# A two-layer graph kernel on one core: layer 1 on pairs of blocks

## The chip, the core and the metric

The kernel runs on one core of a Trainium2 chip. A core has five engines that work side by side, each through its own queue in order: TensorE (PE, matrix products, with the load of the stationary operand listed as PEld), VectorE (DVE), ScalarE (ACT), GpSimd (POOL) and SyncE (SP), which here only starts transfers. Engines wait for one another through semaphores. The metric is the device time of one execution in microseconds (us), as the median of the runs shown; lower is better. Everything is in float32.

## The reference, cut to what is computed

128 graphs have 128 nodes each with 256 features. Layer 0 works on all nodes, layer 1 only on the first 25.

```python
h = relu(layernorm(x))
x = x + L0(h, adj)          # convolution over nodes, neighbour sum, gated unit (GRU)
h = relu(layernorm(x))
x = x + L1(h, adj)

def L1(x, adj):             # groups of 25, 9, 7, 6 and 6 nodes
    fused = 0
    for g, idx in enumerate(GROUPS):
        A = adj[idx, idx] + I
        An = deg(A)**-0.5 * A * deg(A)**-0.5
        h = relu(An @ (x[:, idx] @ W1[g]) + b1[g])      # 256 -> 512
        o = relu(An @ (h @ W2[g]) + b2[g])              # 512 -> 256
        fused[:, idx] += softmax(fusion_w)[g] * o
    return fused
```

The five groups have 25 + 9 + 7 + 6 + 6 = 53 nodes (`NR`); a row of layer 1 is one node of one group of one graph. Since `An @ (x @ W1)` equals `(An @ x) @ W1`, the kernel multiplies with `An` first.

## The kernel before

Layer 0 comes in stages. Stages a and b make the convolution through a short Fourier transform (lines up to 573), in two batches of 64 graphs, with the neighbour sums beside them. Then `stage_c(q)` computes the gates of group q, four graphs at a time, q from 0 to 31 (line 730 on; nearly all its matmuls are recorded at line 758). It ends in `turned` and `returned` (925, 935), which write the new x to DRAM (`x1d`, line 941) from POOL's queue. `fetch(q)` (946) reads the first 32 nodes of these graphs back into `x1` and copies the other nodes to the output.

Layer 1 works on blocks of 16 graphs (`SB`), four groups of q, so there are eight blocks (`NBLK`).
- `rows(q)` (1000) makes the normalized rows `x1h` of four graphs: statistics on VectorE, the power -0.5 on POOL, the subtraction on VectorE, the ReLU on ScalarE.
- `prepare(blk)` (1019) loads the small adjacency, normalizes it and leaves it in two shapes: `ac` for the second use of `An` and `r4` for the first.
- `block(blk)` (1082) does the rest. For each of its four q it multiplies `x1h` with `r4` (`py`, 1094) and evicts into `yz`, which holds the features on the partitions and the rows as columns: half by VectorE (1096), half by ScalarE (1097). For each group g, `first(g)` multiplies 16 x n columns of `yz` with W1 (1111; 8 matmuls, evicted by ScalarE with bias and ReLU at 1113 into `hh`), and `second(g)` multiplies `hh` with W2 (1120; 8 matmuls, copied back over `yz` by VectorE at 1122). So the matmuls of the five groups are 400, 144, 112, 96 and 96 columns wide.
- Its tail is `turn(q)`, `gather(q)` and `fuse(q)` for each q. `turn` transposes `yz` back (1142) and ScalarE copies it into `zt` (1146). `gather` multiplies with `ac` in quarters of the array (1154), VectorE adds the bias row (1157), ScalarE applies the ReLU (1158). `fuse` sums the groups with their weights (1164), VectorE adds that to `x1` (1166), and a DMA writes the output: from POOL's queue (1169), for the last block in pieces from SP and two from ACT (1173).
- W1 of one group (512 KB) is loaded by `load_w1` (996) from SP's queue into one of two buffers, two groups ahead of its use. W2 stays.

The order of instructions on all engines is fixed when the program is built, by `Order` (179): programs yield the cost of the step just recorded on TensorE and a time to stay away; lanes with weights are interleaved by these planned costs. Sets such as `C_DONE`, `R_DONE`, `PY_DONE`, `P_DONE`, `B1_DONE` and `F_DONE` hold a program back in this plan only. On the chip each engine takes its instructions in that order and waits for semaphores of data and of buffers. Layer 1 is one lane (`second`, 1209) with weight 0.2: `prepare` and `block` of each block in turn, two running at a time. When the last gates are done, what is left of that lane follows. The tiles that pass through PSUM under the tag `tmp` share five banks (`ptmp`, 221).

For q = 31 the way is shorter: the result is transposed on TensorE (`po`, 902) and added to `x1` directly (904), without DRAM between.

## Time and profile before

| | |
|---|---|
| median of 3 runs | 1995.26 us (1993.5 to 1996.35) |
| the profiled execution's own time | 1999.49 us |
| span in the profile (first to last instruction) | 1997.7 us |
| mean granted clock of TensorE | 0.998 |
| gates of layer 0 (`p`, line 758), share of the chain that ended last | 40% |
| products with W1 (1111) | 640 records, 107.9 us busy |
| products with W2 (1120) | 640 records, 107.3 us busy |
| `gather` (1154), `fuse` (1164) | 256 records, 21.4 us; 128 records, 20.8 us |
| load of W1 (998) | 40 transfers of 512 KB |

A float32 matmul appears as two records on TensorE. [...] the spacing of starts says what a matmul takes of TensorE's time. In a line of the waits, the waiting instruction stands first, then what it waited for, then total us, times and the longest. In a line of the order of time, the start stands first, then the modelled busy time of the merged instructions. A name such as `pz<-hh,w` is the output and the inputs, followed by partitions x elements.

### The profile page before, as it was taken

Reading aid. Unit: us, or ns where it says so; the run is one execution under the profiler, and the core shown is the slowest. Engines: PE = TensorE matmul, PEld = TensorE weight load, DVE = VectorE, ACT = ScalarE, POOL = GpSimd, SP = SyncE. Lnnn points to the kernel's source line nnn. Section 1 sums busy time; section 2 is a strip of 40 time slices with the busy share of each in tenths; the row PEclk is TensorE's granted clock in tenths of the full one; section 3 lists DMA queues with packets and bytes.
Section 4 is the critical chain, followed back from the end, with each engine's and each line's share of the span. In section 5 each row is a group of like instructions: output and inputs, shape, how many; then the busy total and the mean of one; then the engine's idle time right before and its main releaser. Section 6 shows DMA issues by size and latency. Waiting matters only on the chain.

```text
span 1997.7 us, 33167 instructions
## 1 busy us (share of the span) xinstructions
PE 1950.6 (98%) x12486; PEld 1610.6 (81%) x12486; DVE 1349.5 (68%) x3042; ACT 683.2 (34%) x1547; POOL 650.1 (33%) x898
## 2 busy tenths in 40 slices
PE   7999999999999999999999999999999999999998
PEld 5667888889888888878778878878888888887865
DVE  6775445875433566885885887778678867886652
ACT  3664222444222344222323322232323322322233
POOL 3553665333665111240321233122221321322320
PEclk9999999999999999999999999999999999999999
DMA  9998778654877643542434343443433533433332
GB/s 207 300 283 274 259 265 283 204 164 152 274 254 254 193 127 106 162 106 80 116 95 108 111 111 84 114 109 95 120 110 82 127 105 98 109 101 98 77 90 57
DMA packets 184106, 302.89 MB, mean 152 GB/s; under 512 B 28501, under 2 KB 131994, under 8 KB 183690
## 3 DMA queue, kind: packets, MB, share of 16 engines
q1 hardware_dynamic: 138762, 168.82, 29.1%
q0 software_dynamic: 44800, 131.66, 23.1%
q8 instruction: 99, 1.62, 0.4%
q14 instruction: 61, 0.50, 0.1%
q10 hardware_dynamic: 384, 0.28, 0.1%
HBM read 204.13 MB, written 109.05 MB: 157 GB/s over the span
## 4 chain that ended last, share of the span: by engine, by line
PE 86%; DVE 6%; DMA 4%; issue 1%; ACT 1%; POOL 1%; SPq 0%; DVEq 0%; POOLq 0%; ACTq 0%
PE p L758 40%; PE pa L534 7%; PE ph L1111 5%; PE pm L645 5%; PE pz L1120 5%; PE pc L425 4%; PE pb L534 3%; PE pf L436 3%; PE px L671 3%; PE pi L715 2%; PE pw L480 1%; PE ph L414 1%; PE py L1094 1%; PE pg L1154 1%; PE pse L629 1%
## 5 line engine op out<-in xcount | busy, mean ns | idle before, releaser
L941 POOL DMA_DIRECT2D x1d<-xt x128 | 101.1, 815 | 418.8 <-DVE xt L939 418.4
L840 POOL DMA_DIRECT2D xt<-in_x x128 | 100.2, 790 | 175.4 <-DMA x1d<-xt 168.3
L566 DVE SCALAR_TENSOR_TENSOR y<-pa,kk 128x512 f32<-128x512 f32 x78 | 53.8, 690 | 151.4 <-ACT kk L565 151.4
L534 PE MATMUL pa<-wf,X 128*128 128x256 f32 x640 | 152.2, 381 | 0.0
L758 PE MATMUL p<-th,wrz 128*128 128x256 f32 x512 | 135.4, 387 | 0.0
L758 PE MATMUL p<-tm,wrz 128*128 128x256 f32 x512 | 131.9, 380 | 0.0
L758 PE MATMUL p<-tc,wrz 128*128 128x256 f32 x512 | 131.4, 379 | 0.0
L534 PEld LDWEIGHTS pa<-wf,X 128*128 128x128 f32 x640 | 118.1, 190 | 16.2 <-issue 2.0
L425 PE MATMUL pc<-c1w,hTa 128*128 128x256 f32 x512 | 121.0, 382 | 1.2 <-ACT hTa L416 1.2
L645 PE MATMUL pm<-wmsg,hT 128*128 128x256 f32 x512 | 121.5, 382 | 0.0
L758 PEld LDWEIGHTS p<-th,wrz 128*128 128x128 f32 x512 | 95.1, 191 | 18.7 <-issue 6.3
L1111 PE MATMUL ph<-yz,w 128*128 128x96 f32 (+3 forms) x640 | 107.9, 322 | 1.8 <-DVE yz L1096 1.3
L758 PEld LDWEIGHTS p<-tm,wrz 128*128 128x128 f32 x512 | 97.8, 191 | 13.5
L425 PEld LDWEIGHTS pc<-c1w,hTa 128*128 128x128 f32 x512 | 94.0, 190 | 18.1 <-DVE h L428 4.8
L758 PEld LDWEIGHTS p<-tc,wrz 128*128 128x128 f32 x512 | 97.3, 190 | 14.0 <-issue 1.0
L645 PEld LDWEIGHTS pm<-wmsg,hT 128*128 128x128 f32 x512 | 95.8, 190 | 15.2 <-ACT kk L565 1.4
L727 ACT ACTIVATE xc<-xc,t_bn 128x256 f32<-128x256 f32 x128 | 58.1, 501 | 145.9 <-DVE xc L724 145.9
L1120 PE MATMUL pz<-hh,w 128*128 128x96 f32 (+3 forms) x640 | 107.3, 322 | 0.0
L1111 PEld LDWEIGHTS ph<-yz,w 128*128 128x128 f32 x640 | 86.8, 190 | 22.9 <-issue 15.0
L1113 ACT ACTIVATE hh<-ph,vec 128x96 f32<-128x96 f32 (+3 forms) x160 | 63.2, 401 | 120.5 <-PE ph L1111 111.7
L1120 PEld LDWEIGHTS pz<-hh,w 128*128 128x128 f32 x640 | 86.3, 191 | 17.6
L758 PE MATMUL p<-hTc,wrz 128*128 128x256 f32 x384 | 99.2, 381 | 1.1 <-DVE z L832 1.1
(207 smaller groups left out, 4433.6 us busy)
## 6 DMA issues: line engine op xcount, KB each, us to landing
wf<-wfd SPq DMA_DIRECT2D x160, 256.0 KB
wfd<-ws POOLq DMA_DIRECT2D x64, 320.0 KB, 9.0
yd<-y POOLq DMA_DIRECT2D x80, 256.0 KB, 4.1
yt<-yd SPq DMA_DIRECT2D x64, 320.0 KB
w<-in_W SPq DMA_DIRECT2D x40, 512.0 KB
xa<-in_x SPq DMA_DIRECT2D x128, 128.0 KB
hTd<-hTa POOLq DMA_DIRECT2D x32, 512.0 KB, 6.7
hT<-hTd SPq DMA_DIRECT2D x32, 512.0 KB
```

Source lines behind the costliest of these rows:

```text
L425: nc.tensor.matmul(pc[:, i], hT[:, k, (2 * h + i) * N:(2 * h + i + 1) * N], c1w[:, k], start=(k == 0), stop=(k == 1))
L436: nc.tensor.matmul(pf[:, i, :F * NB], h1[:, 2 * h + i, k * P:(k + 1) * P], fwd, start=True, stop=True)
L534: nc.tensor.matmul(ps, xk(k), WF[f][:, k, s], start=(k == 0), stop=(k == 1))
L645: nc.tensor.matmul(pm[:, i], hT[:, k, j * N:(j + 1) * N], LATE["wmsg"][:, k], start=(k == 0), stop=(k == 1))
L671: nc.tensor.matmul(px[:, dc, i], msgs[h][:, i, dc * P:(dc + 1) * P], aT[:, 2 * h + i], start=True, stop=True)
L727: nc.scalar.activation(xc[:, co, s], xc[:, co, s], AF.Relu, bias=sft["bn2"][:, co:co + 1])
L758: nc.tensor.matmul(ps[:, m], w[:, i, k, m * P:(m + 1) * P], factor(i, x, t), start=first and j == 0, stop=last and j == len(n) - 1, skip_g ...
L840: nc.gpsimd.dma_start(out=xt[a * WIDE:(a + 1) * WIDE].rearrange("p b d c -> p (b d) c"), in_=slices(x[q * GB:(q + 1) * GB])[a])
L941: nc.gpsimd.dma_start(out=slices(x1d[q])[a], in_=xt[a * WIDE:(a + 1) * WIDE].rearrange("p b d c -> p (b d) c"))
L1111: nc.tensor.matmul(ph, w1[:, k, m * P:(m + 1) * P], yz[:, k, :, o:o + n], start=(k == 0), stop=(k == 1))
L1113: nc.scalar.activation(hh[:, m], ph, AF.Relu, bias=v("b1", g * 4 + m))
L1120: nc.tensor.matmul(pz, w2[:, g, m, cc * P:(cc + 1) * P], hs[g][:, m], start=(m == 0), stop=(m == 3))
```

## The change

Layer 1 goes over pairs of blocks, 32 graphs. The groups of 25 and 9 nodes are still multiplied for 16 graphs at a time, for the first half of the pair and then for the second. The groups of 7, 6 and 6 nodes are multiplied once for all 32 graphs, 224, 192 and 192 columns wide, after the second half's rows are in (`TURNS` and `plan`). A pair loads a W1 seven times, where two blocks loaded ten. `yz` holds 32 graphs. The hidden rows `hh` and the turned-back rows `zt` share one tile `hz`, cut in three ways for each. The tail runs once for both blocks: eight `turn`, and four `gather` and four `fuse` that each take two groups of q, eight graphs, at once, with 512 columns in an addition, a ReLU and a fusing matmul. There are three `ac` buffers for two, six `x1h` buffers for eight. The lane runs three programs at a time with weight 0.18. In the last block the output's pieces go 12 from SP and 4 from ACT.

```diff
-        S["ac"] = [pool.tile([P, SB // 2, RP], FP, name=f"ac{i}") for i in range(2)]
+        S["ac"] = [pool.tile([P, SB // 2, RP], FP, name=f"ac{i}") for i in range(3)]
...
-        S["yz"] = pool.tile([P, 2, SB, RP], FP, name="yz")
+        S["yz"] = pool.tile([P, 2, 2 * SB, RP], FP, name="yz")
+        S["hz"] = pool.tile([P, 3, 2 * QS // 4, 2, D], FP, name="hz")
...
-        for t in (*r4, S["yz"][:, 0], S["yz"][:, 1], S["b1"], S["aj"]):
+        for t in (*r4, S["yz"][:, 0, :, NR:], S["yz"][:, 1, :, NR:], S["b1"], S["aj"]):
...
+    TURNS = [(g, h * SB, SB) for h in range(2) for g in range(2)]
+    TURNS += [(g, 0, 2 * SB) for g in range(2, NG)]
+
     def load_w1(n):
 
-        if n < NBLK * NG:
+        if n < NBLK // 2 * len(TURNS):
             S["w1", n] = S["pool"].tile([P, 2, HID], FP, tag="w1", name=f"w1_{n}", bufs=2)
-            nc.sync.dma_start(out=S["w1", n], in_=W1[n % NG].rearrange("(k p) o -> p k o", p=P))
+            nc.sync.dma_start(out=S["w1", n], in_=W1[TURNS[n % len(TURNS)][0]]
+                              .rearrange("(k p) o -> p k o", p=P))
...
-        while not (q in C_DONE and -1 in P_DONE and (q < 8 or q - 8 in PY_DONE)):
+        while not (q in C_DONE and -1 in P_DONE and (q < 6 or q - 6 in PY_DONE)):
...
-        x1h = S["x1h", q] = S["pool"].tile([P, D], FP, tag="x1h", name=f"x1h{q}", bufs=8)
+        x1h = S["x1h", q] = S["pool"].tile([P, D], FP, tag="x1h", name=f"x1h{q}", bufs=6)
...
-        while not (blk - 1 in P_DONE and blk - 2 in {-2, *B1_DONE}):
+        while not (blk - 1 in P_DONE and blk - 3 in {-3, -2, *B1_DONE}
+                   and (blk < 2 or (blk - 1) * QS - 1 in PY_DONE)):
             yield 0.0, 1.0
         pool, pool2, b1 = S["pool"], S["pool2"], S["b1"]
-        ac, r4 = S["ac"][blk % 2], S["r4"][blk % 2]
+        ac, r4 = S["ac"][blk % 3], S["r4"][blk % 2]
...
-    def block(blk):
-        while not (blk in P_DONE and blk - 1 in B1_DONE):
+    def pair(pr):
+        b0 = 2 * pr
+        while not (b0 in P_DONE and (not pr or b0 - 1 in F_DONE)):
...
-        pool, yz, b2row = S["pool"], S["yz"], S["b2row"]
-        w2, ac, r4 = S["w2"], S["ac"][blk % 2], S["r4"][blk % 2]
...
+        yz, b2row, w2, hz = S["yz"], S["b2row"], S["w2"], S["hz"]
+        hf = hz.rearrange("p s i a d -> p (s i a d)")
+        space = [hf[:, :4 * SB * SIZES[0]], hf[:, 4 * SB * SIZES[0]:4 * SB * sum(SIZES[:2])],
+                 hf[:, 4 * SB * sum(SIZES[:2]):]]
+        hs = {}
...
+        def first(i, where):
+            g, s, nb = TURNS[i]
             n, o = SIZES[g], OFFS[g]
-            w1 = S.pop(("w1", blk * NG + g))
-            hh = hs[g] = pool.tile([P, 4, SB, n], FP, tag="hh0" if g == 0 else "hh",
-                                   name=f"hh{blk}_{g}", bufs=1 if g == 0 else 2)
+            w1 = S.pop(("w1", pr * len(TURNS) + i))
+            hh = hs[i] = space[where][:, :4 * nb * n].rearrange("p (m b n) -> p m b n", m=4, n=n)
...
-                ph = ptmp.tile([P, SB, n], FP, tag="tmp", name=f"ph1{blk}_{g}_{m}")
+                ph = ptmp.tile([P, nb, n], FP, tag="tmp", name=f"ph1{pr}_{i}_{m}")
...
-                                     yz[:, k, :, o:o + n], start=(k == 0), stop=(k == 1))
+                                     yz[:, k, s:s + nb, o:o + n], start=(k == 0), stop=(k == 1))
...
-        def second(g):
+        def second(i):
...
-                pz = ptmp.tile([P, SB, n], FP, tag="tmp", name=f"pz1{blk}_{g}_{cc}")
+                pz = ptmp.tile([P, nb, n], FP, tag="tmp", name=f"pz1{pr}_{i}_{cc}")
...
-                    nc.tensor.matmul(pz, w2[:, g, m, cc * P:(cc + 1) * P], hs[g][:, m],
+                    nc.tensor.matmul(pz, w2[:, g, m, cc * P:(cc + 1) * P], hs[i][:, m],
...
-                nc.vector.tensor_copy(yz[:, cc, :, o:o + n], pz)
-
-        for g in range(NG + 1):
-            if g < NG:
-                first(g)
-                yield 5.5 if g == 0 else 1.95, 0.0
-            if g:
-                second(g - 1)
-                yield 5.5 if g == 1 else 1.95, 0.0 if g < NG else 1.0
-            if g < NG:
-                load_w1(blk * NG + g + 2)
-        x1 = X1[blk]
...
+                nc.vector.tensor_copy(yz[:, cc, s:s + nb, o:o + n], pz)
+
+        cost = [max(0.112, nb * SIZES[g] * 0.00084) * 16 for g, _, nb in TURNS]
+        plan = [[(0, 0), (1, 1)], [(2, 0), (3, 1), (4, 2), (5, 0), (6, 2)]]
+        for half in range(2):
+            while b0 + half not in P_DONE:
+                yield 0.0, 0.5
+            for q in range(half * QS, half * QS + QS):
+                yield from rows_in(q)
+            ahead = None
+            for i, where in plan[half]:
+                first(i, where)
+                yield cost[i], 0.0
+                if ahead is not None:
+                    second(ahead)
+                    yield cost[ahead], 0.0
+                load_w1(pr * len(TURNS) + i + 2)
+                ahead = i
+            second(ahead)
+            yield cost[ahead], 1.0
...
-            zt = zts[q] = pool.tile([P, 2, D], FP, tag="zt", name=f"zt{blk}_{q}", bufs=4)
-            nc.scalar.activation(zt, pz, AF.Copy)
-
-        def gather(q):
-            zt = zts[q]
-            pg2 = [ptmp.tile([P, D], FP, tag="tmp", name=f"pg2{blk}_{q}_{s}") for s in range(2)]
-            for a in range(2):
-                for s in range(2):
-                    rows = slice(s * RP, (s + 1) * RP)
-                    nc.tensor.matmul(pg2[s][a * RP:(a + 1) * RP], ac[rows, 2 * q + a],
-                                     zt[rows, a], start=True, stop=True)
+                        yz[:, cc, b:b + 2, :].rearrange("p s r -> p (s r)"), ident)
+            nc.scalar.activation(hz[:, q // 2 % 3, q % 2], pz, AF.Copy)
+
+        def gather(h):
+            zt, ac = hz[:, h % 3], S["ac"][(b0 + h // 2) % 3]
+            pg2 = [ptmp.tile([P, 2, D], FP, tag="tmp", name=f"pg2{pr}_{h}_{s}")
+                   for s in range(2)]
+            for i in range(2):
+                for a in range(2):
+                    for s in range(2):
+                        rows = slice(s * RP, (s + 1) * RP)
+                        nc.tensor.matmul(pg2[s][a * RP:(a + 1) * RP, i],
+                                         ac[rows, 4 * (h % 2) + 2 * i + a],
+                                         zt[rows, i, a], start=True, stop=True)
             for s in range(2):
-                nc.vector.tensor_add(zt[:, s], pg2[s], b2row)
-            nc.scalar.activation(zt, zt, AF.Relu)
-
-        def fuse(q):
-            zt = zts.pop(q)
-            pf = ptmp.tile([P, D], FP, tag="tmp", name=f"pfu{blk}_{q}")
+                nc.vector.tensor_add(zt[:, :, s], pg2[s],
+                                     b2row[:, None, :].to_broadcast([P, 2, D]))
+                nc.scalar.activation(zt[:, :, s], zt[:, :, s], AF.Relu)
+
+        def fuse(h):
+            zt, blk = hz[:, h % 3], b0 + h // 2
+            x1 = X1[blk][:, 2 * (h % 2):2 * (h % 2) + 2]
+            pf = ptmp.tile([P, 2, D], FP, tag="tmp", name=f"pfu{pr}_{h}")
             for s in range(2):
-                nc.tensor.matmul(pf[s * 2 * WIDE:(s + 1) * 2 * WIDE], s2w, zt[:, s],
+                nc.tensor.matmul(pf[s * 2 * WIDE:(s + 1) * 2 * WIDE], s2w, zt[:, :, s],
                                  start=True, stop=True)
-            nc.vector.tensor_add(x1[:, q], x1[:, q], pf)
-            b0 = blk * SB + q * GB
-            if blk < NBLK - 1:
-                nc.gpsimd.dma_start(out=out[b0:b0 + GB, :WIDE], in_=x1[:, q])
-                return
-            for j in range(GB):
-                eng = nc.scalar if q == QS - 1 and j % 2 else nc.sync
-                eng.dma_start(out=out[b0 + j, :WIDE], in_=x1[j * WIDE:(j + 1) * WIDE, q])
-
-        for what, q in ((turn, 0), (turn, 1), (turn, 2), (gather, 0), (turn, 3), (gather, 1),
-                        (gather, 2), (fuse, 0), (gather, 3), (fuse, 1), (fuse, 2), (fuse, 3)):
-            what(q)
-            if (what, q) == (gather, QS - 1):
-                B1_DONE.add(blk)
-            yield {turn: 0.45, gather: 0.5, fuse: 0.5}[what], 0.5
-        F_DONE.add(blk)
+            nc.vector.tensor_add(x1, x1, pf)
+            for i in range(2):
+                g0 = (b0 * QS + 2 * h + i) * GB
+                if blk < NBLK - 1:
+                    nc.gpsimd.dma_start(out=out[g0:g0 + GB, :WIDE], in_=x1[:, i])
+                    continue
+                for j in range(GB):
+                    eng = nc.scalar if h % 2 and j % 2 else nc.sync
+                    eng.dma_start(out=out[g0 + j, :WIDE], in_=x1[j * WIDE:(j + 1) * WIDE, i])
+
...
+        for what, i in ((turn, 0), (turn, 1), (turn, 2), (gather, 0), (turn, 3), (turn, 4),
+                        (gather, 1), (turn, 5), (fuse, 0), (gather, 2), (turn, 6), (turn, 7),
+                        (fuse, 1), (gather, 3), (fuse, 2), (fuse, 3)):
+            what(i)
+            if what is gather and i % 2:
+                B1_DONE.add(b0 + i // 2)
+            if what is fuse and i % 2:
+                F_DONE.add(b0 + i // 2)
+            yield {turn: 0.45, gather: 1.0, fuse: 1.0}[what], 0.5
 
...
-    second = [setup_1()] + [part(blk) for blk in range(NBLK) for part in (prepare, block)]
+    second = [setup_1()]
+    for pr in range(NBLK // 2):
+        second += [prepare(2 * pr), prepare(2 * pr + 1), pair(pr)]
...
-              Lane(second, ahead=2, weight=0.2))
+              Lane(second, ahead=3, weight=0.18))
```

## Prediction

> **What bounds the kernel now.** I read the page first, then the waits of TensorE, then stretches of the run, then single stretches in order of time.
>
> ```profile
> span 1997.7 us, 33167 instructions
> ## 1 busy us (share of the span) xinstructions
> PE 1950.6 (98%) x12486; PEld 1610.6 (81%) x12486; DVE 1349.5 (68%) x3042; ACT 683.2 (34%) x1547; POOL 650.1 (33%) x898
> ```
>
> TensorE (PE) is busy for 98% of the span and the next engine for 68%. So matmul time that goes shortens the run, and work saved on the other engines does not. The stretches below (length, then busy time by engine) show where there is any slack: none between 1400 and 1800 us, where gates of layer 0 and pieces of layer 1 alternate, and 13 us in the last 95 us, where layer 1 is alone.
>
> ```profile
> 1400.00:1600.00 200.00, 199.02 (x1257) 164.96 (x1256) 152.80 (x338) 59.20 (x130) 54.05 (x77) 1.00 0.42 109
> 1600.00:1800.00 200.00, 200.00 (x1303) 166.71 (x1305) 155.09 (x337) 59.35 (x129) 48.35 (x71) 1.00 0.38 102
> 1903.00:1997.70 94.70, 81.65 (x534) 57.23 (x533) 38.23 (x106) 32.13 (x73) 14.84 (x26) 0.98 0.26 72
> ```
>
> TensorE's waits (total, times, longest) are small; no load of the gate stage or of W1 is among them.
>
> ```profile
> PE p L758 <- DVE r L880: 7.1, 8, 2.4
> ...
> PE py L1094 <- ACT x1h L1015: 2.0, 1, 2.0
> ...
> PE py L1094 <- DVE x L1166: 1.1, 1, 1.1
> ...
> PE po L902 <- DVE zr L896: 0.9, 1, 0.9
> ```
>
> "Busy" does not say how fast, so I take prices from start to start in the order of time. This is block 7, alone at the end (start, modelled busy time):
>
> ```profile
> 1964.14 5.54 PE L1120 MATMUL pz<-hh,w 128*128 128x400 f32 x16
> 1969.52 1.95 PE L1111 MATMUL ph<-yz,w 128*128 128x112 f32 x16
> 1971.30 2.13 PE L1120 MATMUL pz<-hh,w 128*128 128x144 f32 x16
> 1973.26 1.92 PE L1111 MATMUL ph<-yz,w 128*128 128x96 f32 x16
> 1975.02 1.96 PE L1120 MATMUL pz<-hh,w 128*128 128x112 f32 x16
> 1976.82 1.96 PE L1111 MATMUL ph<-yz,w 128*128 128x96 f32 x16
> 1978.61 3.72 PE L1120 MATMUL pz<-hh,w 128*128 128x96 f32 x32
> ```
>
> Each product is two records. One record of 400 columns costs 5.38/16 = 0.336 us, of 144 columns 1.96/16 = 0.1225, of 112 columns 1.78/16 = 0.111, of 96 columns 1.76/16 = 0.110. In the gates, 256 columns cost 0.864/4 = 0.216 (starts 1786.58, 1787.44). From 144 to 400 the price is a line of 0.00083 us a column; below 128 it is flat at 0.11. The three small groups lie on the flat.
>
> **Part 1, the three small groups on 32 graphs.** Before, one block spends 1.78 + 1.80 (7 nodes) and 1.76 + 1.79 + 3.57 (twice 6 nodes) = 10.7 us, a pair 21.4. After, a pair has 32 records of 224 columns and 64 of 192. No row shows these widths; they lie between rows of 144 and 256, so the line gives 0.189 and 0.163: 6.05 + 10.43 = 16.5. That is 4.9 us a pair, **19.7 us** over four, all on the engine that bounds.
>
> [...] I take the trace: 19.7.
>
> The groups of 25 and 9 nodes keep their width (400 and 144): nothing. ScalarE and VectorE lose instructions: 96 evictions of hidden rows at 0.34 to 0.35 become 48 of about 0.43, and 48 copies of 0.26 to 0.28 become 24: some 16 us on engines with room, counted at nothing. W1 is loaded 28 times instead of 40; what its wait holds up on SP's queue are loads that TensorE never waited for, so fewer of them gain nothing either.
>
> **Part 2, the tail on two groups of four graphs at once.** Rows for it:
>
> ```profile
> 1903.80 1.09 PE L1154 MATMUL pg<-zt,ac 64*64 64x256 f32 x16
> 1904.82 0.65 PE L1164 MATMUL pfu<-zt,s2w 128*64 128x256 f32 x4
> ```
>
> One gather costs 0.59 from start to start, two in a row 1.02. One fuse costs 0.58, of which its columns are 2 x 0.216 = 0.43 and 0.15 is the change of tiling. A fuse of 512 columns has no row: between 0.86 (columns alone) and 1.16 (two of before); nearest is 0.86 + 0.15 = 1.01. A pair: 8 x (0.59 + 0.58) - 4 x (1.02 + 1.01) = 1.2 us, times four = 5.0. Between gates, the first product behind a gather or a fuse takes 0.54 where others take 0.43 (1900.84, 1901.43, 1901.97); a pair has eight fewer such returns: 0.9, for the three pairs that lie among gates 2.6. Together **7.6 us**.
>
> **Part 3, what becomes late at the end.** Before, layer 1 lagged two blocks: when the last gate product ended (1903.7), blocks 6 and 7 were still to do, and block 6 hid the way of the last rows (q = 31) into layer 1. In the order of the changed program, after the last gate product stand the second products of block 6's groups 0 and 1, `pr` of block 7, then `py_4`, `py_5`, `po`, `py_6`, `py_7`, and only then block 7's groups. Block 7's rows are wanted at once. I follow the queues, t = 0 at the last gate product:
> - TensorE: `pz` 400 wide to 5.4, `pr` to 6.4, `pz` 144 wide to 8.4.
> - VectorE in order: the copy of that 400-wide product ends at 6.1, because the finish of dc = 1 (3 x 0.72) is queued behind it: 8.2; four copies of `r4` at 0.38: 9.7; two copies: 10.3; the finish of dc = 0: 12.4; `zr`: 12.8.
> - So `py_4` starts at 9.9 rather than 8.4, `po` at 12.95. Behind `po`: its addition (14.0), a copy, statistics (0.42 + 0.18 + 0.15), the power on POOL with its way (0.86, from 1915.49 to 1916.35), subtraction 0.40, ReLU 0.42: `py_7` at 17.1, the first product of block 7 at 18.5. TensorE's work in it is 11.6: **6.9 us idle**. Before, the same rows waited 0.4 + 1.15 + 0.9 + 1.25 + 0.5 = 4.2.
>
> The last tail: `turn`, `gather` and `fuse` of two blocks without gates between. On ScalarE the copy of turn 3 stands behind both ReLUs of gather 0 (copy and ReLU 0.53 to 0.63, addition of 512 columns 0.60 to 0.69, as L875 and L1158 have them). Stepping through: gather 1 ends at 6.2 after the first turn, gather 2 at 9.4, gather 3 at 13.05, the last fuse at 15.6 with 11.75 of work: 3.9 idle, where one tail of before had 1.1 (8.20 - 7.13 from 1982.0 to 1990.2).
>
> ```profile
> 1987.91 7.60 SPq L1173 DMA_DIRECT2D out<-x  x14
> ```
>
> The run ends by SP: 14 output DMAs at 0.54 us, then 2.2 to the end of the span. After, SP issues 12, none before fuse 2 of block 7 is added (15.0): 15.0 + 12 x 0.54 + 2.2 = 23.8, so 8.2 behind the last matmul instead of 7.5.
>
> Sum of idle time: 6.9 + 3.9 + 8.2 = 19.0 against 13.0 (94.7 - 81.65): **+6.0 us**.
>
> **Part 4, waits among the gates.** In the new order a pair's second half asks for its rows one group of gates apart (groups 14 to 17, 24 to 25), so these groups carry little of layer 1 between their last, short products. Where gates had little beside them before, `p` waited 0.59 to 0.67 for `r` (834.59, 867.87, 1003.99). Some four such groups: 2.4. Bounds: 0 (the wait is met elsewhere) to 8 (a wait of 2 for `x1h`, as seen once, at four more `py`). I take **+2.5**, near the rows. The new waits of `prepare` (three `ac`, six `x1h`) hold only plan time; SP's and POOL's orders keep their count of loads per group.
>
> **Sum**: -19.7 - 7.6 + 6.0 + 2.5 = **-18.8 us**. The profiled execution (1999.49, span 1997.7) would be 1980.7; it stands 4.2 above the median of the runs, so I forecast 1995.26 - 18.8 = **1976.5 us**.
>
> **Rivals.**
> - *The end costs more*: the power or the ReLU queued later, and the clock. [...] Between `py_6` (14.1) and `py_7` (17.1) lie 3.0 us. In the trace, 1.25 us of idle left the clock at 1.00, and it shows 0.78 only in the last 7.5 us, without matmuls. [...] I take nothing. With it, a tail 3 us longer and Part 4 at 6: 1985. Chance 0.15.
> - *More gained*: gates hide Part 4, a fuse costs 0.86, the end 4: about 1971. Chance 0.12.
> - *No change*: [...] Against it: 96 and 112 columns cost the same. Chance 0.05.
> - *Slower*: rows come late. A pair's second half needs rows just made; TensorE is in order, so a `py` that waits holds every gate behind it. Twelve such `py` in three pairs at the 1.95 us seen at 1049.76 make 23.4: 1976.5 - 2.5 + 23.4 = 1997.4; at 2.5 us, 2004. It decides from about 1.8 us each. Against it: from `xt` added (1885.17) to the row in place is 15.9 us (issue at 1896.42, 4.6 to landing), plus 2.5 to the ReLU, while the plan leaves 24.5; and the same pattern in block 1 (`py_1` to `py_3`, one a group, before 1000 us) shows no wait. Chance 0.07.
>
> The forecast keeps 0.61. A measurement of this kernel tells some 0.2%, 4 us, from no change; faster by more than that 0.88, within 0.05, slower 0.07. Range: costs at their good ends (-2.5, -2, -2.4) and run scatter give 1968; the first rival with scatter 1988.
>
> **What would show it.** Records of 192 and 224 columns start every 0.163 and 0.189 us; 16 fuses at 1.0; `p` behind `r` L880 at about 10 us in total; waits of `po` and `py` near 7 us after the last gate; the span ends 8 us after the last matmul. I am wrong if the small groups of a pair still take over 20 us, or if `py` behind `x1h` sums to over 15 us.

## The result, and the profile after

| | before | after |
|---|---|---|
| median of 22 runs each, side by side | 1999.01 us (1993.5 to 2004.56) | 1993.56 us (1985.45 to 1999.38) |
| ratio after / before | | 0.9961, 95% interval 0.9949 to 0.9972 |
| span of the profiled execution | 1997.7 us | 1991.4 us |
| mean granted clock of TensorE over the runs | 0.9969 (93 runs) | 0.9947 (28 runs) |

The changed kernel is 5.5 us faster by the medians, 7.8 us by the ratio. The forecast was 18.8 us. (The 93 runs of the kernel before are those beside the experiments; 28 are the 22 and 6 more.)

The head of the page after the change: TensorE has 448 records fewer and still bounds.

```profile
span 1991.4 us, 32103 instructions
## 1 busy us (share of the span) xinstructions
PE 1935.7 (97%) x12038; PEld 1595.8 (80%) x12038; DVE 1341.2 (67%) x2970; ACT 670.8 (34%) x1499; POOL 651.3 (33%) x898
```

The stretches (length, then busy time of PE, PEld, DVE, ACT and POOL, then the granted clock, DMA share, GB/s):

```profile
1400.00:1600.00 200.00, 198.60 (x1244) 163.94 (x1243) 149.14 (x319) 60.90 (x129) 55.89 (x80) 1.00 0.39 101
1600.00:1800.00 200.00, 199.82 (x1207) 168.40 (x1205) 144.27 (x310) 56.78 (x123) 43.44 (x63) 1.00 0.37 101
1903.00:1991.40 88.40, 72.12 (x378) 50.78 (x376) 32.25 (x67) 25.17 (x52) 9.29 (x14) 0.96 0.23 63
```

Between 1400 and 1800 us TensorE stays full. Alone at the end it is idle for 88.4 - 72.1 = 16.3 us instead of 13.0, and the clock of that stretch is 0.96 instead of 0.98. The waits of TensorE (total us, times, longest):

```profile
PE p L758 <- DVE r L880: 5.4, 10, 0.7
...
PE py L1105 <- ACT x1h L1020: 5.3, 3, 2.8
...
PE pg L1172 <- ACT hz L1162: 2.0, 3, 1.0
...
PE py L1105 <- DVE r L1084: 1.4, 1, 1.4
...
PE po L902 <- DVE zr L896: 1.3, 1, 1.3
```

`py` behind `x1h` has grown from 2.0 to 5.3 us: 2.8 of it is the last `py` of the run, 1.95 is the wait that was there before. The gates' wait for `r` at L880 came ten times for 5.4 us; before it came eight times for 7.1, of which a single wait was 2.4.

The small groups of the last pair, in the order of time:

```profile
1947.66 3.61 PE L1121 MATMUL ph<-yz,w 128*128 128x224 f32 x16
...
1953.07 2.76 PE L1121 MATMUL ph<-yz,w 128*128 128x192 f32 x16
1955.67 3.19 PE L1131 MATMUL pz<-hz,w 128*128 128x224 f32 x16
1958.69 3.63 PE L1121 MATMUL ph<-yz,w 128*128 128x192 f32 x16
1962.15 5.37 PE L1131 MATMUL pz<-hz,w 128*128 128x192 f32 x32
```

Rows have 16 records, the last 32; the distance to the next start gives the price (1951.11 and 1967.36 follow the first and the last row). The second products (`pz`) cost 3.02/16 = 0.189 us at 224 columns and 5.21/32 = 0.163 at 192: the forecast to the digit. The first products (`ph`) do not: 224 columns cost 3.45/16 = 0.216; of two groups with 192 columns, one costs 2.60/16 = 0.163 and the other 3.46/16 = 0.216. All records of a form, with their busy time and mean ns:

```profile
L1121 PE MATMUL ph<-yz,w 128*128 128x192 f32 x128 | 25.6, 353 | 0.0
L1131 PE MATMUL pz<-hz,w 128*128 128x192 f32 x128 | 21.9, 326 | 0.0
L1121 PE MATMUL ph<-yz,w 128*128 128x224 f32 x64 | 14.4, 378 | 0.0
L1131 PE MATMUL pz<-hz,w 128*128 128x224 f32 x64 | 12.8, 352 | 0.0
```

The same numbers of records, the same columns and the same weights' size: `ph` takes 3.7 + 1.6 = 5.3 us more than `pz`. (A record's mean, 326 to 378 ns, is longer than the spacing of starts, 163 to 216 ns: records overlap.)

To see where the rest went I added up both traces from start to start on TensorE, every gap over 0.1 us counted as idle (us; "gates" are the records of line 758):

| | forecast | before | after | measured |
|---|---|---|---|---|
| all products with W1 and W2 | -19.7 | 203.5 | 190.1 | -13.4 |
| `gather` and `fuse` | -5.0 | 38.0 | 33.3 | -4.7 |
| gates (cheaper returns behind a `gather` or `fuse`) | -2.6 | 894.3 | 895.0 | +0.7 |
| idle among gates | +2.5 | 13.1 | 16.3 | +3.2 |
| idle after the last gate, and the end behind the last matmul | +6.0 | 13.5 | 16.9 | +3.4 |
| first gate to end of span, with all the rest | -18.8 | 1322.6 | 1310.4 | -12.2 |
| start to first gate | 0 | 675.1 | 681.0 | +5.9 |

(The terms hold what the clock took in their stretch.) Up to the first gate the two programs issue the same instructions on every engine, in the same order. What differs ahead of it in these two executions is when two transfers came in, and windows of 3.41 us at half clock: the trace before has one such window ahead of its last matmul, at 779 us; the trace after has five, at 171, 372, 785, 1041 and 1932 us. Two of the five lie ahead of the first gate, and two among the gates, where the trace before has its one.

The difference ahead of the first gate may be more than chance. In the three kept profiles of the kernel before (one with its rows placed, as told below) the first gate starts at 674.1 to 675.4 us and no window at half clock lies ahead of it. In the eleven profiles of the changed kernel and its variants it starts at 675.8 to 683.2 us, behind one to four such windows. No run here shows why.

### The profile page after: what moved, and what is told of

The parts are those of the page before. It is cut to its first block, busy times and chain, and to the rows that moved or that the text cites. A ratio compares the mean times of both kernels' runs of the same rounds, so it can differ in the third digit from the quotient of the medians.

```text
span 1991.4 us, 32103 instructions
## 1 busy us (share of the span) xinstructions
PE 1935.7 (97%) x12038; PEld 1595.8 (80%) x12038; DVE 1341.2 (67%) x2970; ACT 670.8 (34%) x1499; POOL 651.3 (33%) x898
## 4 chain that ended last, share of the span: by engine, by line
PE 85%; DVE 9%; DMA 2%; ACT 1%; issue 1%; SPq 0%; POOL 0%; DVEq 0%; ACTq 0%; POOLq 0%
PE p L758 38%; PE pa L534 7%; PE ph L1121 5%; PE pm L645 5%; PE pc L425 5%; PE pz L1131 4%; PE pb L534 3%; PE pf L436 3%; PE px L671 3%; PE pi L715 2%; PE pw L480 2%; PE ph L414 1%; PE py L1105 1%; PE pse L629 1%; PE pd L660 1%
## 5 line engine op out<-in xcount | busy, mean ns | idle before, releaser
L534 PEld LDWEIGHTS pa<-wf,X 128*128 128x128 f32 x640 | 118.1, 190 | 16.2 <-issue 2.0
L758 PEld LDWEIGHTS p<-tc,wrz 128*128 128x128 f32 x512 | 98.1, 192 | 13.5
L758 PEld LDWEIGHTS p<-tm,wrz 128*128 128x128 f32 x512 | 97.9, 191 | 13.5
L1121 PE MATMUL ph<-yz,w 128*128 128x400 f32 (+3 forms) x448 | 102.2, 381 | 0.5 <-DVE yz L1108 0.5
L529 POOL TENSOR_TENSOR wf<-wf 128x512 f32<-128x512 f32 x78 | 98.7, 1265 | 0.0
L758 PE MATMUL p<-xm,wrz 128*128 128x256 f32 x384 | 98.5, 379 | 0.0
L758 PE MATMUL p<-xc,wrz 128*128 128x256 f32 x384 | 98.5, 379 | 0.0
L1131 PE MATMUL pz<-hz,w 128*128 128x400 f32 (+3 forms) x448 | 96.1, 368 | 0.7 <-DVE yz L1133 0.7
```

The lines of the kernel that those rows point to most:

```text
L529: nc.gpsimd.tensor_tensor(WF[f][:, :, 2], WF[f][:, :, 0], WF[f][:, :, 1], ALU.add)
L534: nc.tensor.matmul(ps, xk(k), WF[f][:, k, s], start=(k == 0), stop=(k == 1))
L758: nc.tensor.matmul(ps[:, m], w[:, i, k, m * P:(m + 1) * P], factor(i, x, t), start=first and j == 0, stop=last and j == len(n) - 1, skip_g ...
L1121: nc.tensor.matmul(ph, w1[:, k, m * P:(m + 1) * P], yz[:, k, s:s + nb, o:o + n], start=(k == 0), stop=(k == 1))
L1131: nc.tensor.matmul(pz, w2[:, g, m, cc * P:(cc + 1) * P], hs[i][:, m], start=(m == 0), stop=(m == 3))
```

## Experiments

After the result I had three theories. The first: the first products pay for something in `yz` that their width does not show. The second: the waits at the end cost more than their idle time, because the clock falls behind them. The third, their rival: 32 graphs gain less than their records say, and something all along the run takes it back. (In the expectations, A and B are named anew for each run.) Times are compared through the ratio to the kernel before, which ran beside each (medians 1999.21, 2000.64, 2001.07 and 2001.92 us in the four batches).

**The kernel before again**, unchanged, to see how far its times scatter and where a second profile has its first gate.

> The kernel before, unchanged, for its own granted clocks and a second profile. Question: the changed kernel's profile reaches its first gate product at 681.0 us, the one of before at 675.1, with the same instructions up to there, and shows TensorE's clock halved for 3.4 us five times before its last matmul, where before shows one. Theory C (lottery of idle windows): the first part and the count of halved windows vary from run to run in both kernels, mean clock 0.992 to 0.998, and each halved window costs about 1.7 us; this profile has its first gate anywhere from 675 to 682. Rival: the change itself makes the first part slower; then this profile has its first gate at 675 again and clocks stay at 0.998.

2002.26 us, ratio 1.0006 (0.9994 to 1.0019): no difference, within 0.19% at most. In its profile the first gate starts at 675.4 us, and the clock is 0.998. That is what the rival expected (the change itself makes the first part slower), so theory C is not confirmed; one profile does not refute it either. Its runs are not as good as its profiles: the mean clock over these 14 runs is 0.9967.

**Small groups on 16 graphs again**, all else as changed.

```diff
-    TURNS = [(g, h * SB, SB) for h in range(2) for g in range(2)]
-    TURNS += [(g, 0, 2 * SB) for g in range(2, NG)]
+    TURNS = [(g, h * SB, SB) for h in range(2) for g in range(NG)]
...
-        plan = [[(0, 0), (1, 1)], [(2, 0), (3, 1), (4, 2), (5, 0), (6, 2)]]
+        plan = [[(5 * h + g, w) for g, w in enumerate((0, 1, 2, 0, 1))] for h in range(2)]
```

> The changed kernel with the three small groups taken for 16 graphs again (ten W1 a pair); the common tail, the buffers and the order of the pair stay. It prices the wide products alone. By the forecast (19.7 us for the columns) it is 19.7 us slower than the changed kernel. By theory A (the first products stream short runs of 6 and 7 columns out of yz and lose 5.2 us of it) it is about 14.5 us slower, some 2008. By a rival in which the loss lies in clock and waits alone, 19 or more. Against before: by the forecast's other terms (tail -7.6, end and waits +8.5) about +1; by the tail as the profile has it (about -4.5) +3 to +7.

1998.49 us, ratio 0.9997 (0.9984 to 1.001): only 4.9 us slower than the changed kernel by the medians, 7.2 by the ratios. But its trace says that two things changed: the products cost 13.6 us more, and the idle time after the last gate fell from 8.8 to 3.0 us, because more small products were left to fill the waits there. The comparison was not clean; it is made again below.

**Rows of x in another order.** In `yz` a graph has 64 columns of 4 bytes. The first product of a small group reads 7 or 6 adjacent columns of each graph: columns 34 to 40, 41 to 46, 47 to 52. Cut into pieces of four columns, the fast group (41 to 46) touches two pieces a graph, the two slow ones three. So I placed the groups 6, 6, 7, 9, 25, beginning at columns 0, 6, 12, 19 and 28: two pieces for each small group.

```diff
-OFFS = [sum(SIZES[:i]) for i in range(NG)]
+PLACES = [3, 4, 2, 1, 0]
+OFFS = [sum(SIZES[p] for p in PLACES[:PLACES.index(g)]) for g in range(NG)]
...
-    row_node = [n for g in GROUPS for n in g]
-    row_group = [i for i, g in enumerate(GROUPS) for _ in g]
+    row_node = [n for p in PLACES for n in GROUPS[p]]
+    row_group = [p for p in PLACES for _ in GROUPS[p]]
```

> The changed kernel with the 53 rows of a graph in another order, groups of 6, 6, 7, 9, 25 nodes from columns 0, 6, 12, 19, 28 instead of 41, 47, 34, 25, 0. No work is added or removed. In the changed kernel's trace a record of a first product with 224 columns starts every 0.216 us and one of the two with 192 every 0.218, while the other 192 and all second products (contiguous) have 0.163 and 0.189. Theory A [...]: here each run of 6 and 7 touches two pieces, so the first products go to 0.163 and 0.189 everywhere, and the run is 5.2 us shorter, about 1988. Rival A2 (short runs as such cost, or the tile's bank): spacings stay 0.216 and 0.218 and the time stays at 1993.5.

1986.78 us, ratio 0.9938 (0.992 to 0.9956), below the changed kernel by 6.8 us by the medians and by 4.6 by the ratios. The forms of its first products:

```profile
L1122 PE MATMUL ph<-yz,w 128*128 128x192 f32 x128 | 22.1, 325 | 0.0
...
L1122 PE MATMUL ph<-yz,w 128*128 128x224 f32 x64 | 12.8, 352 | 0.0
```

192 columns fall from 25.6 to 22.1 us, 224 from 14.4 to 12.8, the level of `pz`: 5.1 us of TensorE's time. Runs at columns 6 to 11 and 12 to 18 cross borders of 8 and 16 columns and take no more than `pz` (325 and 352 ns against 326 and 352), so those borders are not it.

**The opposite order**, to see the price move: 7, 6, 25, 9, 6 nodes (`PLACES = [2, 3, 0, 1, 4]`).

> The changed kernel with the rows of x placed in the order 7, 6, 25, 9, 6 nodes, so that the 7 start at column 0 (two pieces of four columns), the first 6 at column 7 (three pieces) and the other 6 at column 47 (three pieces). Theory A [...]: records of 224 columns in the first product come down from 0.216 to 0.189, and both groups of 192 columns take 0.218, also the one that took 0.163 before. Rival B (the price depends on which group or which column range it is, not on the pieces): the 224 columns stay at 0.216, and one group of 192 stays at 0.163. The time is within the scatter of one look either way (theory A: +1.8 us).

1988.72 us in a single run, from which the time tells nothing. The same two forms:

```profile
L1122 PE MATMUL ph<-yz,w 128*128 128x192 f32 x128 | 29.0, 381 | 0.0
...
L1122 PE MATMUL ph<-yz,w 128*128 128x224 f32 x64 | 12.8, 352 | 0.0
```

The 7 nodes, now at column 0, are cheap (12.8), and both groups of 6, now at columns 7 and 47, are dear: 29.0 us, 3.4 above the changed kernel, where one of them was cheap. The price follows the place, not the group. The three orders put runs of 6 or 7 at eight places: five are cheap (columns 0 to 5, 0 to 6, 6 to 11, 12 to 18, 41 to 46), three dear (7 to 12, 34 to 40, 47 to 52). Of pieces of 2 to 8 columns, only those of four tell them apart: two pieces in each cheap run, three in each dear one. Per graph and record, a dear run takes 0.216/32 = 6.75 ns, for 6 columns as for 7. A third of it, 2.25 ns, is my estimate for one piece. By it two pieces take 4.5 ns, less than the cheap runs took (0.163/32 = 5.1 and 0.189/32 = 5.9), so there the columns would bind.

Another reading fits the short runs as well. The dear runs have a piece of which they use a single column (34 to 40 end with one, 47 to 52 have one at each end). If such a piece took as long as two columns, both runs would cost eight columns, and 32 of them as much as 256 columns, which is 0.216 too. Longer runs speak against it. With the rows placed, the 9 nodes (19 to 27) begin with a single column, and their records start every 0.124 us instead of 0.1225, where a full column more would make 0.136. The 25 nodes end with one in both orders above this one and cost 0.339; here (13 to 37) they do not, and cost 0.336.

**The same placing in the kernel before.**

> The kernel before, with the rows of x placed as in the run with aligned rows and nothing else changed. Theory A [...]: spacing of these records stays at 0.110 to 0.113, and the time stays within 0.1% of 1999. Rival B (the placing saves time whatever the width, through the other reads of these rows, or through the matmuls of other widths): the gain of 6.8 us shows here too, 1992.

1999.64 us, ratio 0.9997 (0.9985 to 1.0009): nothing. Block 7 of this run, first products of 112 and 96 columns:

```profile
1965.57 1.93 PE L1112 MATMUL ph<-yz,w 128*128 128x112 f32 x16
1967.34 2.14 PE L1121 MATMUL pz<-hh,w 128*128 128x144 f32 x16
1969.31 1.92 PE L1112 MATMUL ph<-yz,w 128*128 128x96 f32 x16
1971.07 1.96 PE L1121 MATMUL pz<-hh,w 128*128 128x112 f32 x16
```

1.77/16 = 0.111 and 1.76/16 = 0.110, as before. At 16 graphs, three pieces cost 16 x 6.75 = 108 ns by the estimate, just under the flat price of 0.110; the pieces were touched there too and did not show. So, by the estimate, the flat part hid not only columns, as the forecast had it, but also this second price. (The flat part has rows in the trace before at 96, 112 and 128 columns alone: 0.110, 0.111 and 0.11, the last from four transposes at 1902.40 us that take 0.60 where one takes 0.27. What sets it, no run here tested.)

**The last pair's first products held** until the last gate product is issued, so that they fill the waits behind it.

```diff
             for i, where in plan[half]:
+                while pr == NBLK // 2 - 1 and NQ - 1 not in G_DONE:
+                    yield 0.0, 0.5
                 first(i, where)
```

> The changed kernel in which the last pair's first products of block 6 wait, in the plan, for the last gates, so that some 14 us of layer 1 stand between the last gate product and the rows of the last group. Theory B (what became late at the end): the waits of po, py and ph behind the last gate (1.4, 1.3, 2.8 and 0.5 us in the changed kernel's profile) fall to under 1 in all, and the halved clock after them (1.7 us) mostly goes: 5 to 7 us shorter, 1987 to 1989. Rival: the gates of the last groups lose their filling and wait for r instead, or the waits return at py_4 behind r4: under 2 us shorter.

1983.91 us, ratio 0.9926 (0.991 to 0.9941), below the changed kernel by 9.6 us by the medians and by 7.0 by the ratios. The order of time after the last gate, first of the changed kernel, then of this one (in brackets the wait ahead):

```profile
1921.55 2.12 PE L1131 MATMUL pz<-hz,w 128*128 128x144 f32 x16
1925.10 1.70 PE L1105 MATMUL py<-r,x1h 128*128 128x212 f32 x8 [1.42 <-DVE r L1084]
1928.05 0.41 PE L902 MATMUL po<-cst,zr 128*128 128x128 f32 x2 [1.25 <-DVE zr L896]
1928.30 0.88 PE L1105 MATMUL py<-r,x1h 128*128 128x212 f32 x4
1931.98 1.54 PE L1105 MATMUL py<-r,x1h 128*128 128x212 f32 x4 [2.80 <-ACT x1h L1020]
1933.99 8.46 PE L1121 MATMUL ph<-yz,w 128*128 128x400 f32 x32 [0.47 <-DVE yz L1108]
1942.29 5.53 PE L1131 MATMUL pz<-hz,w 128*128 128x400 f32 x16
```

```profile
1919.35 2.12 PE L1131 MATMUL pz<-hz,w 128*128 128x144 f32 x16
1921.31 2.31 PE L1105 MATMUL py<-r,x1h 128*128 128x212 f32 x12
1924.15 0.98 PE L1105 MATMUL py<-r,x1h 128*128 128x212 f32 x4 [0.52 <-ACT x1h L1020]
1925.60 7.65 PE L1121 MATMUL ph<-yz,w 128*128 128x400 f32 x32 [0.47 <-DVE yz L1108]
1933.09 5.54 PE L1131 MATMUL pz<-hz,w 128*128 128x400 f32 x16
```

Waits of 1.42 + 1.25 + 2.80 + 0.47 = 5.9 us become 0.52 + 0.47; the idle time after the last gate falls by 4.9 us. The mean clock over the runs of the two kernels with held products (this and the one with all three edits) is 0.9969 in 11 runs, that of the kernel before; the changed kernel's is 0.9947. A third kernel with held products, the next one, has 0.9962 in 22 runs.

What the clock did at that place in the changed kernel, in three stretches (the third number from the end is the granted clock):

```profile
1918.60:1932.26 13.66, 8.19 (x40) 5.91 (x39) 9.38 (x24) 1.41 (x4) 0.55 (x1) 1.00 0.00 1
1932.26:1935.67 3.41, 2.94 (x7) 1.68 (x7) 1.33 (x2) 0.35 (x1) 0.00 (x0) 0.50 0.00 0
1935.67:1942.50 6.83, 6.83 (x32) 4.69 (x31) 0.00 (x0) 3.42 (x7) 0.00 (x0) 1.00 0.10 19
```

A window of 3.41 us at 0.50 follows the one that held the wait of 2.80 us. Five profiles of kernels whose end waits like this one's (the changed kernel twice, its rows in the two other orders, its tail's order below) have such a window between 1918 and 1937 us, three of them two in a row. The five profiles in which products or fillers stand in these waits have none between the last gate and the last matmul. The kernel before has one there in one of its three profiles (at 1905 us). From its length and its clock I estimate that a window at half clock with TensorE at work costs 3.41/2 = 1.7 us.

**Held, with the small groups on 16 graphs**: the clean form of the second experiment, to be compared with the run just told.

> The kernel with held products of the last pair, and its three small groups on 16 graphs again: the same work waits at the end in both. Theory A (the first run with 16 graphs was only 4.9 us slower than the changed kernel because its order filled the waits at the end, which the changed kernel's did not): with the end filled in both, 16 graphs cost the 13 to 14 us that the spacing of the records gives, 1983.9 + 13.6 = 1997.5. Rival B (32 graphs gain only some 5 us, something else takes the rest back all along the run): 1989.

1997.75 us, ratio 0.999 (0.9978 to 1.0002): 0.0064, or 12.8 us, above the held kernel. The records differ by 14.4 us (189.1 against 203.5), the idle time at the end by 0.9 the other way. The third theory falls: 32 graphs gain what their records say, some 13 us.

**Fillers in the waits of the end**: the same clock question without an earlier start of anything.

```diff
             py = ptmp.tile([P, 2, GB, NR], FP, tag="tmp", name=f"py{pr}_{q}")
+            for _ in range({4: 5, 5: 5, 7: 12}.get(q, 0) if pr == NBLK // 2 - 1 else 0):
+                nc.tensor.matmul(py[:, 0].rearrange("p j r -> p (j r)"), ident,
+                                 w2[:, 0, 0, :GB * NR], start=True, stop=True)
```

> The changed kernel with 22 idle matmuls of 212 columns (about 0.18 us each) written ahead of three products in the last pair: 5 ahead of py_4, 5 ahead of py_5 and 12 ahead of py_7, each into the buffer that the real product then overwrites. They fit into waits that TensorE has there anyway (1.42, 1.25 and 2.80 us), so the work waited for comes no earlier. Theory A (these waits cost twice: once as idle time, and once as windows at half clock that they bring on): the mean granted clock over the runs rises from 0.9944 to about 0.997 and the time falls by some 5 us, to 1989, though matmuls were added. Rival B (the lower clock of the changed kernel has another source): clock and time stay, 1993.6, or up to 1 us more where a filler ends behind its wait.

1991.73 us, ratio 0.9958 (0.9946 to 0.997); the changed kernel run beside it had 0.9954 (0.9936 to 0.9972):

> The changed kernel again, beside the run that fills its waits. It should come out at the time of its other runs, 1993.6, with a mean granted clock of about 0.9944 over its runs (the kernel before: 0.997).

No difference. My fillers were twice as long as I had said: 0.18 us is one record, and each matmul is two.

```profile
1917.36 2.12 PE L1134 MATMUL pz<-hz,w 128*128 128x144 f32 x16
...
1924.33 0.38 PE L902 MATMUL po<-cst,zr 128*128 128x128 f32 x2
1924.55 0.88 PE L1108 MATMUL py<-r,x1h 128*128 128x212 f32 x4
1925.27 4.46 PE L1105 MATMUL py<-w,cst 128*128 128x212 f32 x24
1929.57 0.88 PE L1108 MATMUL py<-r,x1h 128*128 128x212 f32 x4
...
1938.41 5.54 PE L1134 MATMUL pz<-hz,w 128*128 128x400 f32 x16
```

From `po` to the last `py` it is 5.24 us here and was 3.93; from the product ahead of `py_4` to `po` it is 6.97 (1917.36 to 1924.33) and was 6.50 (1921.55 to 1928.05). So 1.31 + 0.47 = 1.8 us were added to the path. Yet from the first row above to the last it is 21.05 us, and in the changed kernel 20.74 (1921.55 to 1942.29; its second profile has 20.73): only 0.3 more. The profile has no window at half clock there, so by estimate (1.8 - 0.3) the window was worth some 1.5 us. The runs do not show it: the mean clock was 0.9956 (19 runs), and 0.9957 in the six runs of the changed kernel beside them, and the intervals of the two times would hide 1.5 us. The forecast of 5 us fell: by these runs the waits are not the source of most of the clock's loss over the whole run.

**The tail's turns ahead of its gathers**, so that ScalarE's copies do not stand behind ReLUs.

```diff
-        for what, i in ((turn, 0), (turn, 1), (turn, 2), (gather, 0), (turn, 3), (turn, 4),
-                        (gather, 1), (turn, 5), (fuse, 0), (gather, 2), (turn, 6), (turn, 7),
+        for what, i in ((turn, 0), (turn, 1), (turn, 2), (turn, 3), (gather, 0), (turn, 4),
+                        (turn, 5), (gather, 1), (fuse, 0), (turn, 6), (turn, 7), (gather, 2),
                         (fuse, 1), (gather, 3), (fuse, 2), (fuse, 3)):
```

> The changed kernel with turns 3, 5 and 7 of the tail ahead of gathers 0, 1 and 2, so that ScalarE's copies of these turns no longer stand behind the ReLUs of a gather. Theory A (TensorE's waits in the last tail, 2.9 us in the changed kernel, come from ScalarE's order): these waits fall to about 1 us and the run is about 2 us shorter, 1991.5. Rival B (the chain gather, addition, ReLU, fuse sets the tail whatever the order): the waits move to the last gather and the fuses, their sum stays within 0.5 us, and the time stays at 1993.5.

1989.13 us, ratio 0.9951 (0.9933 to 0.997): by the ratio 2 us better than the changed kernel's 0.9961, within the intervals. The trace shows the idle time after the last gate down from 8.8 to 6.7, and 1.0 of it given back behind the last matmul (9.1 for 8.1 us). The last transfers of the changed kernel, then of this one:

```profile
1982.77 6.19 SPq L1195 DMA_DIRECT2D out<-x  x12
```

```profile
1980.40 7.26 SPq L1195 DMA_DIRECT2D out<-x  x12
```

SP issues its 12 output transfers one behind the other, here 0.605 us each for 0.516.

**All three edits** (placing, holding, tail's order).

> The changed kernel with three edits at once: the rows of x placed [...] (-6.8 us when it stood alone), the last pair's first products held until the last gate product (-9.6 alone), and the tail's turns ahead of its gathers (about -2). Theory A (the three save time at different places): they add up, 1993.6 - 6.8 - 9.6 - 2 = 1975. Rival B (the held products gained only through a clock that happened to be higher in those runs): 1993.6 - 6.8 - 4.9 (the idle time alone) - 2 = 1980.

1976.8 us, ratio 0.9889 (0.9869 to 0.9909). By the ratios the three edits alone gained 4.6, 7.0 and 2.0 us, together 13.6, and here it is 14.4: they add up. This kernel is 1.1% faster than before, 0.7% faster than the changed one. Idle time after the last gate is 1.7 us, and the mean clock over its six runs is 0.9970.

**Its remaining windows at half clock filled.** Its profile still has three such windows ahead of the last matmul:

```profile
169.63:173.04 3.41, 3.41 (x15) 3.41 (x14) 0.62 (x3) 1.26 (x3) 0.00 (x0) 0.50 0.89 271
780.62:784.03 3.41, 3.41 (x11) 2.87 (x12) 1.87 (x4) 2.76 (x5) 0.84 (x2) 0.50 0.89 236
1036.62:1040.03 3.41, 3.41 (x10) 2.70 (x8) 1.76 (x4) 0.35 (x1) 0.00 (x0) 0.50 0.00 0
```

```diff
+            for _ in range(3 if j == GB - 1 and q in (10, 11, 30) else 0):
+                nc.tensor.matmul(pds[0][:, 1], ident, ident, start=True, stop=True)
             nc.tensor.matmul(pds[j][:, 0], lr[rows, 0], lr[rows, 1], start=True, stop=True)
+        for _ in range(4 if q == 0 else 0):
+            nc.tensor.matmul(pds[0][:, 1], ident, ident, start=True, stop=True)
...
+            for _ in range(4 if (pr, q) == (0, QS * 2 - 1) else 0):
+                nc.tensor.matmul(py[:, 0].rearrange("p j r -> p (j r)"), ident,
+                                 w2[:, 0, 0, :GB * NR], start=True, stop=True)
```

> The kernel with the three edits together (1976.8, mean clock over its runs 0.9970), with 17 idle matmuls in the waits beside which its profile shows windows at half clock (168, 371, 781 and 1037 us): 4 of 128 columns (0.22 us each) ahead of the transposes of the first adjacency, 3 ahead of the last of four pd products in calls 10, 11 and 30, 4 of 212 columns (0.36 us each) ahead of the last py of the first pair. All fit into waits of 0.6 to 2.7 us that are there anyway. Theory A (the windows at half clock come from these waits, and each costs about 1.7 us): windows at these places go from the profile, the mean clock rises to 0.998 or more, and the time falls by 2 to 5 us, to 1972 to 1975. Rival B (windows come whatever fills the waits, or cost no time): the same clock and 1976.8, or up to 1 us more.

1976.26 us in four runs, ratio 0.9869 (0.9852 to 0.9886): by the median nothing, by the ratio 4 us, and the intervals overlap. (The one at 371 us that the expectation names stood in the profile of the changed kernel, not in this one's.) In the profile of the filled kernel the windows at 781 and 1037 us are gone:

```profile
163.84:174.08 10.24, 6.24 (x28) 4.86 (x29) 1.12 (x2) 2.14 (x5) 0.00 (x0) 0.50 0.50 164
780.00:790.00 10.00, 9.97 (x110) 8.39 (x109) 7.24 (x13) 5.43 (x10) 3.13 (x4) 1.00 0.38 106
1036.00:1044.00 8.00, 7.46 (x47) 6.29 (x49) 5.62 (x11) 1.50 (x4) 0.00 (x0) 1.00 0.00 0
```

But in this execution two transfers came late at 165 us (TensorE waited 3.8 and 2.3 us), three windows at half clock followed each other, and a further one stands at 20 us. Three of its four runs had a clock of 0.998, this one 0.995 and the longest time, 1982.29. Neither that these fillers move the windows nor that they gain time is shown: of the 13 other profiles, none of which has fillers at these two places, six have no window near 781 us and seven none near 1037 us.

## Why the prediction was wrong

The direction was right, the size was a third (medians) to two fifths (ratio) of the forecast. Neither of its own signs of being wrong came: the small groups of a pair take 17.7 us, not over 20, and `py` behind `x1h` sums to 5.3, not over 15. By its own steps:

- **Part 1, price of 192 and 224 columns: the step that failed in the sum.** "No row shows these widths; they lie between rows of 144 and 256, so the line gives 0.189 and 0.163". It holds for the second products, which stream `hz` in one piece. For the first products of 224 columns and of one group of 192 the price is 0.216: 64 x 0.027 + 64 x 0.054 = 5.2 us on the bounding engine. The two rows from which the line was drawn (400 and 144 columns, at 1964.14 and 1971.30) are second products, which stream `hh` in one piece; their price was carried over to first products, which stream short runs of `yz`. By the estimate of 2.25 ns, first products of these widths would hardly have shown it: 400 columns are runs of 25 in seven pieces, 7 x 2.25 = 15.8 ns for 25 columns that take 21 anyway; 144 are runs of 9 in three pieces, 6.75 ns for 7.7. The first products with runs of 6 and 7, where three pieces cost more than the columns (6.75 ns for 5.1 and 5.9), lay on the flat part before, where the price of pieces (108 ns by the estimate) is just under the floor (110). The placed rows give 5.1 us back in the records, and 4.6 (ratios) to 6.8 (medians) in time. Another 0.8 us of this term is the clock's: first products at half clock at 1934 us (8.30 us to the next start, where the held kernel has 7.49).
- **Part 2.** 16 fuses at 1.0: 1974.22 to 1975.23, 1.01 as forecast, and -4.7 for -5.0. Of the 2.6 us for fewer returns among gates the two traces show nothing (894.3 and 895.0 us), but the clock hides it: the trace after has two windows at half clock among its gates, the trace before one. The profiles with none there have 892.9 us for the kernel before (its second) and 891.9, 892.0 and 891.8 for the changed one (rows placed, in the opposite order, tail's order). So some 1.0 us came of 2.6.
- **Part 3.** Each wait came where it was put and a little shorter: `py_4` 1.42, `po` 1.25, `py_7` 2.80, `ph` 0.47, together 5.9 for 6.9; the tail 2.9 for 3.9; the end behind the last matmul 8.1 from its start, almost as before. The term was +3.4 for +6.0.
- **Part 4.** +3.2 for +2.5, or up to 6: idle time among gates is 13.1 us in the trace before, but 10.6 and 10.3 in two more of its profiles (one with its rows placed), and 16.3 and 16.2 in two of the changed kernel. The named wait is a small part of it. Against the second profile of the kernel before, `p` behind `r` L880 went from 4.5 us (7 times) to 5.4 (10 times), where I had set 10 us as the sign; behind `z` L832 it went from 1.1 to 2.7, behind `r` L872 from 0.3 to 1.8.
- **The clock, which I took as nothing: the second step that failed.** The first rival had the clock in it, and against it I took a row in which 1.25 us of idle time left the clock at 1.00. What a lower clock would cost (a part of that rival's 1985 us) no row showed at that time. The trace after shows windows of 3.41 us at half clock (0.50) behind stretches of 3.41 us in which TensorE was idle for 2.80 us (to 1932.26, at the end), 1.95 (to 1041.39) and 3.23 (to 170.99). A row with 1.25 us could not speak for a wait of 2.8. Nor was it so that the trace before showed a lower clock only in its last 7.5 us: the window at 779 us stands in it, behind one with 0.89 us idle, and the stretch around it has 0.99:

```profile
730.00:1000.00 270.00, 264.10 (x1714) 217.39 (x1707) 203.88 (x463) 92.19 (x196) 76.67 (x119) 0.99 0.44 121
```

Within the changed kernel, runs with a clock lower by 0.001 are 2.0 us longer; 0.9969 - 0.9947 is then some 4.5 us. (The two sets of its runs differ: 0.9944 in 22, 0.9957 in six.) One to two windows of it (1.7 to 3.4 us by the estimate above) belong to the end, by the profiles. Where the rest comes from stays open. The fillers left the clock as it was; two held kernels had that of the kernel before, the third only 0.9962. The profiles point ahead of the first gate too, where the changed kernel and its variants always have a window and the kernel before has none, but a profile is one execution.

Together: a straight line through time and clock of the runs (28 of the changed kernel, 93 of the kernel before) gives 1987.5 and 2000.2 us at a clock of 0.997, so -12.7 at an equal clock. At the clocks that the runs had, some 4.5 less is left, about the ratio's -7.8 (the medians have -5.5). Of the 11.0 us that are missing from 18.8, the pieces took 5.2, which experiments show, and the clock 4.5, of which only the part at the end has a shown place; the other 1.3 is the balance of smaller terms, returns that came in part and more waits among gates against an end that cost less.

The rival "no change" was nearer to the measured time than the forecast, but not because wider products gain nothing: 32 graphs gain 12.8 us against 16. "Slower" did not come: of the twelve `py` in three pairs one waited 1.95 us, as one had before, and one 0.56.

## What to carry to other kernels

A price that is flat can hide prices below it: when a change takes a product off a floor, ask what else it streams (here, how many pieces of four columns each short run touches: 0.216 us a record with three, 0.163 and 0.189 with two), not only how many columns. Try another place for short runs; it cost four lines here. When idle time on the bounding engine gathers into one long wait (here 2.80 us, with 3.41 us at half clock behind it), price it with the clock behind it, and keep work back to fill it rather than run it early.

## What the runs showed of the hardware

- The time of a first product on short runs of `yz` went with the place of the runs: a record with 32 runs of 6 columns takes 0.216 us where each run touches three pieces of four columns, and 0.163 where it touches two; with runs of 7 it takes 0.216 and 0.189. From 0.216/32/3 I estimate 2.25 ns a piece, as a limit beside the columns. Borders of 8 and 16 columns showed no price (325 and 352 ns a record, as the second products).
- Windows at half clock (0.50) in these traces last 3.41 us, or whole multiples (6.83, 10.24), and the starts in one trace are whole multiples of 3.413 us apart: 170.99, 372.37, 785.39, 1041.39 and 1932.26 us in the trace after. With this trace and the one before cut at these multiples from 12 us on, ahead of the last matmul, half clock followed the three stretches in which TensorE was idle for 3.23, 2.80 and 1.95 us, and not the next, with 1.91 us (at 1311.78 us in the trace before). Below it both occur: half clock followed one with 1.52 us (at 368.96, after) and two with 0.90 (781.97, after) and 0.89 (775.89, before), and did not follow others with 1.66 (164.91, before) and 1.49 (1905.70, before). A wait of 2.0 us for `x1h` had half clock behind it where it lay in one stretch (1.95 us of it from 1037.97, after), and none where a border cut it (1.16 and 0.80 us idle from 1045.54 and 1048.96, before).
- With 22 idle matmuls in the waits of the end, the window at half clock there was gone and by estimate some 1.5 us with it (one profile, against five of waiting kernels that have the window). The mean clock of the runs did not show it.
